# Layer 0's bias moved from the residual x to the half that the graph is applied to

## The chip, the cores and the metric

The kernel runs on one core of a Trainium2 chip. The metric is the device time of one execution in microseconds, lower is better. Five engines work side by side, each through its own queue in order: TensorE (PE: matmuls, and PEld: its weight loads), VectorE (DVE), ScalarE (ACT), GpSimd (POOL) and SyncE (SP), which starts the transfers. They wait for one another through semaphores.

## The reference

The input x has 64 batches of 256 nodes with 512 features; adj is a symmetric 256 x 256 graph of zeros and ones. Two residual layers with a layer norm follow each other. Layer 0 is a graph convolution, layer 1 masked attention with 8 heads of 64:

```python
Wi, Wj = (W[:, :Din], W[:, Din:])
mi = jnp.einsum('bkd,od->bko', x, Wi)
mj = jnp.einsum('bkd,od->bko', x, Wj)
a = adj.astype(x.dtype)
deg = a.sum(axis=1)
out = deg[None, :, None] * (mi + b) + jnp.einsum('ij,bjo->bio', a, mj)
...
x = _layernorm(x + _L0_gnn_ref(x, adj, L0_gnn_W, L0_gnn_b), axis=-1)
x = _layernorm(x + _L1_gnn_ref(x, adj, Wq, bq, Wk, bk, Wv, bv, Wo, bo), axis=-1)
```

The bias b of layer 0 comes in as deg times b. Since deg is the row sum of a, deg times b is also the graph applied to a matrix whose rows are all b: deg * (mi + b) + a @ mj equals deg * mi + a @ (mj + b).

## The kernel before

Everything is in float32, except the graph product. A tile has 128 partitions; one batch of x is `xh`, [128, 2, 512], two row tiles t. Batches go in pairs (NB = 2), 32 groups g. All large products are done in seven block products in place of eight, with sums of blocks made beforehand (`xS`, `hS`, `oS` hold S1 to S4) and factors of the weights made beforehand (`w0` for layer 0, streamed `factor` tiles for layer 1).

The main loop over g overlaps layer 1 of group g with layer 0 of group g+1. In a round, attention goes over eight pairs of heads, two at a time: `values` (pav) for the last two, `divide_two` (den on PE, the reciprocal L882 on DVE, the transfers to `spread`, later the aoT product on POOL, L844), `scores` (ps on PE; the mask add L805 on DVE, the exponential L809 on ACT, pk L812 on POOL). Between these stand the pieces of layer 0 of the next pair, from `l0_steps`; then come the output product, the finishing norms, and q, k, v of the next group. Matmuls and most calls marked `in_order` keep the order in which they are written; each engine runs its queue in order.

For one batch, `l0_steps` has seven products into four banks of PSUM, x, w, y and z, and then the graph:
- step 1 and 3 fill bank x (u1 is its copy on ACT, L530, and x's sum is added into xh, scaled by the degree, on DVE, L520); step 2 fills bank w, added into xh likewise.
- step 4 fills y; u2 = y + u1 on DVE (L542).
- step 5 fills z; the first half of the second row tile of mj is copied out of z by ACT (L547).
- step 6 adds to y; u3 = y + u1 on DVE (L551); mj's second row tile gets u3 added on POOL (L552); u3, scaled, is added into xh (L520).
- step 7 adds to z; the first row tile of mj is z + u2 on DVE (L561).
- after a row tile of mj, `split` makes hi (a rounded copy on ACT, L524) and lo (the rest, on POOL, L525).
- `neighbours` multiplies the graph with hi and lo (bank pa); `take` adds pa into xh (L575) and starts the norm.

Step 7 goes into the bank that step 5's copy reads, so it waits for that copy. `sum_x` makes xS of the second batch of a pair with four DVE operations (L477 to L480) just after step 7 of the first batch.

The bias comes into x: `degb` is deg times b, made once on DVE (L371); `add_bias` adds it to xh of each batch on POOL (L374), before layer 0 adds its products. b itself is a broadcast tile `b_bc` from a shared pool.

Of the kernel before, what the change touches and what calls it, by code (L numbers as in the profile page):

```python
# [8 lines left out]
F32 = mybir.dt.float32  # L9
# [3 lines left out]
ALU = mybir.AluOpType  # L13
# [3 lines left out]
P = 128  # L17
# [207 lines left out]
def unshifted_path(ctx, tc, flag, x, adj, wiT, wjT, b0, wqT, bq, wkT, bk, wvT, bv, woT, bo, out):  # L225
# [16 lines left out]
    nc = tc.nc  # L242
    B, N, D = x.shape
    NT = N // P
# [3 lines left out]
    NB = 2  # L248
    NG = B // NB
# [6 lines left out]
    const = ctx.enter_context(tc.tile_pool(name="const", bufs=1))  # L256
# [3 lines left out]
    p4 = ctx.enter_context(tc.tile_pool(name="p4", bufs=4))  # L260
# [8 lines left out]
    def bank(name):  # L269
        return ps_m.tile([P, 512], F32, tag="mm", name=name)  # L270

    def score_banks(name):
        return ps_s.tile([P, 2, 512], F32, tag="sc", name=name)
# [8 lines left out]
    def in_order(ins):  # L282

        tc.keep_in_program_order(ins)
# [4 lines left out]
    def matmul(*args, **kw):  # L289
        in_order(nc.tensor.matmul(*args, **kw))  # L290
# [5 lines left out]
    xh = {}  # L296
# [3 lines left out]
            xh[b] = p6.tile([P, NT, D], F32, tag="xh", name="xh")  # L300
            nc.sync.dma_start(out=xh[b], in_=x[b].rearrange("(t p) d -> p t d", p=P))

    b_bc = p4.tile([P, D], F32, tag="u", name="b_bc")
    xB, hB = {}, {}

    def load_xB(b):
# [31 lines left out]

    graph = const.tile([P, NT, N], F32R, name="graph")
    maskT = const.tile([P, NT, N], F32, name="maskT")  # L340
    degb = const.tile([P, NT, D], F32, name="degb")
    a = p2.tile([P, NT, N], F32, tag="pe", name="a")
    aT = p3.tile([P, NT, N], F32, tag="pk", name="aT")
    deg = small.tile([P, NT], F32, tag="deg", name="deg")
# [16 lines left out]
    def check_graph():  # L361
# [3 lines left out]
        in_order(nc.vector.tensor_tensor(exact, aT, graph.bitcast(F32), ALU.not_equal))  # L365
        in_order(nc.vector.tensor_reduce(inexact, exact.rearrange("p t n -> p (t n)"), AX.X, ALU.max))
        in_order(nc.vector.tensor_scalar(maskT, aT, 0.0, MASK, ALU.is_equal, ALU.mult))

    def degree_bias():
        for t in range(NT):  # L370
            in_order(nc.vector.tensor_scalar(degb[:, t, :], b_bc, deg[:, t:t + 1], None, ALU.mult))  # L371

    def add_bias(b):
        in_order(nc.gpsimd.tensor_tensor(xh[b], xh[b], degb, ALU.add))  # L374


    def load_bias(b, name):
# [86 lines left out]
    def norm_apply(t, below, rstd, order=anywhere):  # L464
        shift = small.tile([P, 1], F32, tag="shift", name="shift")
        order(nc.scalar.activation(shift, below, AF.Identity, scale=rstd))  # L466
        order(nc.scalar.activation(t, t, AF.Identity, bias=shift, scale=rstd))  # L467
# [34 lines left out]
    def l0_steps(b):  # L502
        banks, k = {}, {}

        def product(name, left, n, first):
            if first:
                banks[name] = bank("po")
            for c in range(2):
                matmul(banks[name], left[:, c, :], w0[:, n, c, :], start=(first and c == 0),
                                 stop=(c == 1), skip_group_check=True)  # L510

        def raw(t, h):
            return xT[b][:, 2 * h:2 * h + 2, t * P:(t + 1) * P]

        def keeper(name):
            k[name] = p3.tile([P, D], F32, tag="lu", name=name)
            return k[name]

        def add_scaled(t, src):
            nc.vector.scalar_tensor_tensor(xh[b][:, t, :], src, deg[:, t:t + 1], xh[b][:, t, :],  # L520
                                           ALU.mult, ALU.add)

        def split(t):
            nc.scalar.copy(k["hi"][:, t, :], k["mj"][:, t, :])  # L524
            nc.gpsimd.tensor_tensor(k["lo"][:, t, :], k["mj"][:, t, :], k["hi"][:, t, :].bitcast(F32),  # L525
                                    ALU.subtract)

        def step1():
            product("x", raw(0, 0), B11, True)
            nc.scalar.copy(keeper("u1"), banks["x"])  # L530

        def step2():
            product("w", raw(1, 1), T4, True)
            add_scaled(1, banks["w"])

        def step3():
            product("x", raw(0, 1), B21, False)
            add_scaled(0, banks["x"])

        def step4():  # L540
            product("y", xS[b]["S2"], T2, True)
            nc.vector.tensor_add(keeper("u2"), banks["y"], k["u1"])  # L542

        def step5():
            product("z", xS[b]["S1"], T1, True)
            k["mj"] = p1.tile([P, NT, D], F32, tag="mj", name="mj")
            nc.scalar.copy(k["mj"][:, 1, :], banks["z"])  # L547

        def step6():
            product("y", xS[b]["S3"], T3, False)  # L550
            nc.vector.tensor_add(keeper("u3"), banks["y"], k["u1"])  # L551
            nc.gpsimd.tensor_tensor(k["mj"][:, 1, :], k["mj"][:, 1, :], k["u3"], ALU.add)  # L552

            k["hi"] = p1.tile([P, NT, D], F32R, tag="hi", name="hi")
            k["lo"] = p1.tile([P, NT, D], F32R, tag="lo", name="lo")
            split(1)
            add_scaled(1, k["u3"])

        def step7():
            product("z", xS[b]["S4"], B22, False)  # L560
            nc.vector.tensor_add(k["mj"][:, 0, :], banks["z"], k["u2"])  # L561
            split(0)

        stats = {}

        def neighbours():
            k["pa"] = score_banks("pa")
            for i in (1, 0):
                for n, (j, part) in enumerate((j, part) for j in (1, 0) for part in ("hi", "lo")):
                    matmul(k["pa"][:, i, :], graph[:, j, i * P:(i + 1) * P], k[part][:, j, :],  # L570
                           start=(n == 0), stop=(n == 2 * NT - 1))

        def take(t):
            r = xh[b][:, t, :]
            in_order(nc.vector.tensor_add(r, k["pa"][:, t, :], r))  # L575
            stats[t] = norm_stats(r, in_order)

        def give(t):
            norm_apply(xh[b][:, t, :], *stats[t], in_order)


        return [step1, step2, step3, step4, step5, step6, step7, neighbours, lambda: take(1), lambda: take(0),
                lambda: give(1), lambda: send_h(b, 1), lambda: give(0), lambda: send_h(b, 0)]

# [310 lines left out]
    def layer0(g):  # L895

        b1, b2 = NB * g, NB * g + 1

        def item(f, *args):
            return lambda: f(*args)  # L900

        p, q = l0_steps(b1), l0_steps(b2)
        return [p[:3] + [item(turn_x, b2)] + p[3:4],
                p[4:7] + [item(sum_x, b2), item(add_bias, b2)] + q[:1],
                p[7:10], p[10:] + q[1:3],
                q[3:6] + [item(turn_h, b1)] + q[6:7],
                q[7:], [item(turn_h, b2)]]

    def run(steps):
        for s in steps:  # L910
            s()
# [4 lines left out]
    def order_of(name):  # L916
        return [(name, n) for n in RIGHT]

    for g in range(-1, NG - 1):
        o, q, k, v = (order_of(name) for name in ("wo", "wq", "wk", "wv"))  # L920
# [18 lines left out]
    p, q = l0_steps(0), l0_steps(1)  # L939
    run([p[0], p[2], p[4], p[3]])  # L940
    turn_x(1, "hB")
    degree_bias()
    add_bias(0)
    turn_graph()
    run([p[1], p[5], q[0], p[6], q[2]])
    add_bias(1)
    sum_x(1)
    run(q[1:2] + p[7:11] + q[3:5] + p[12:13])
    make_factors(wqT, "wq", raw_q)
# [9 lines left out]
    k = second_late(qk_steps(0, kT, "kT", bk_sb, bkd, True))  # L959
# [13 lines left out]
    run(v[2:3])  # L973
    turn_x(2)
    sum_x(2)
    add_bias(2)
    run(v[3:5])
    make_factors(woT, "wo", raw_o)
    load_x(3)
# [2 lines left out]
    for g in range(NG - 1):  # L982
        load_x(NB * (g + 2))
        load_x(NB * (g + 2) + 1)
        work = layer0(g + 1)
        run(work[0])
        for w in range(2, NB * NC, 2):
            values(g, w - 2)
            values(g, w - 1)
            multiply()  # L990
            divide_two(g, w - 1)
            scores(g, w)()
            if w == 4:
                run(work[2])
            later = scores(g, w + 1)
            later()
            run(work[w // 2 if w < 4 else w // 2 + 1])
        w = NB * NC - 2
        values(g, w)
        values(g, w + 1)  # L1000
        multiply()
        o = o_steps(g)
        q = second_late(qk_steps(g + 1, qT, "qT", bq_sb, bqd))
        k = second_late(qk_steps(g + 1, kT, "kT", bk_sb, bkd, True))
        v = second_late(v_steps(g + 1, True))
        neighbours, take1, take0, give1, send1, give0, send0 = work[SLOTS + 1]
        divide_two(g, w + 1)
        run([o[0], neighbours, take1, take0, q[0], give1, send1, o[1], give0, send0, multiply,
             *left_steps(oS[g], in_order), k[0], q[1], k[1]])
        run(o[2:6] + work[SLOTS + 2] + [v[0], o[6], v[1]])  # L1010
        end = finish_steps(g)
        k = with_output_bias(g + 1, k)[2:]
        run(q[2:5] + end[:1] + q[5:6] + end[1:2] + q[6:7] + end[2:3] + k[:1] + end[3:4] + k[1:] + end[4:] + v[2:3])
        turn_x(NB * (g + 2))
        sum_x(NB * (g + 2))
        if g + 2 < NG:
            add_bias(NB * (g + 2))
        run(v[3:5])
        run([scores(g + 1, 0), scores(g + 1, 1)])
        run(v[5:])  # L1020
# [3 lines left out]
    g = NG - 1  # L1024
# [89 lines left out]
```

## Time and profile before

The median of three runs is 3117.14 us (3116.6 to 3118.32); the profiled execution has a span of 3113.4 us.

| Engine | Busy us | Share of the span | Instructions |
|---|---|---|---|
| PE | 3071.3 | 99% | 14598 |
| PEld | 2117.8 | 68% | 14598 |
| DVE | 2148.5 | 69% | 3234 |
| ACT | 1007.8 | 32% | 1925 |
| POOL | 1520.8 | 49% | 1255 |

The rows of operations that the change touches, from the groups by line (busy us in total, mean ns of one):

| Line | Engine | What | Times | Busy us | Mean ns |
|---|---|---|---|---|---|
| L374 | POOL | xh + degb, 128x1024 | 64 | 157.7 | 2464 |
| L547 | ACT | mj from bank z, 128x512 | 64 | 36.8 | 575 |
| L561 | DVE | mj = z + u2, 128x512 | 64 | 43.9 | 686 |
| L552 | POOL | mj + u3, 128x512 | 64 | 111.6 | 1743 |
| L812 | POOL | pk, 128x512 | 256 | 322.3 | 1275 |
| L371 | DVE | degb, 128x512 | 2 | 1.9 | 966 |

A busy share is a mean over the whole span. An engine's idle time says something about the total only where another engine, in the end PE, waits for it. In the timeline every row has a start (us from the start of the span), a length, the engine, the line, the operation with its tiles, and in brackets how long the engine was idle before it and what ended that.

### The profile page before, as it was taken

The numbers are of one execution on the slowest core, as the hardware profiler recorded it, in microseconds if no ns is written. First come the engines' busy times: TensorE is split into PE (matmuls) and PEld (weight loads), VectorE is DVE, ScalarE is ACT, GpSimd is POOL, SyncE is SP. The second block draws the span as 40 slices with busy tenths as digits, with TensorE's granted clock in tenths as the row PEclk, the third lists the DMA queues.
The fourth block names the chain that finished last, engine by engine and source line by source line (L and its number), as shares of the span: only waits on it lengthen the run. The fifth ranks groups of instructions, "written<-read, shape, count | busy, mean of one in ns | idle before, by whom it ended". The sixth has DMA issues, their size and how long they took to land. (4 is left out here: it accounts for less than half of the span.)

```text
span 3113.4 us, 42777 instructions
## 1 busy us (share of the span) xinstructions
PE 3071.3 (99%) x14598; PEld 2117.8 (68%) x14598; DVE 2148.5 (69%) x3234; ACT 1007.8 (32%) x1925; POOL 1520.8 (49%) x1255
## 2 busy tenths in 40 slices
PE   7999999999999999999999999999999999999998
PEld 5667766677766677666776667766677766677665
DVE  6776676766777667676667676667766667767665
ACT  2333333323333333333233332333333333323332
POOL 2544445544545445454454554454544546445453
PEclk9999999999999999999999999999999999999999
DMA  7345544455444555445553445544455444555333
GB/s 256 121 143 156 166 124 134 128 157 165 141 124 123 157 166 152 117 131 149 157 166 118 131 134 157 165 139 123 127 155 169 146 118 127 154 162 160 116 111 98
DMA packets 410395, 447.28 MB, mean 144 GB/s; under 512 B 40896, under 2 KB 300224, under 8 KB 409792
## 3 DMA queue, kind: packets, MB, share of 16 engines
q1 hardware_dynamic: 410176, 444.50, 48.3%
q8 instruction: 120, 1.97, 0.3%
q14 instruction: 99, 0.81, 0.1%
HBM read 340.79 MB, written 70.25 MB: 132 GB/s over the span
## 5 line engine op out<-in xcount | busy, mean ns | idle before, releaser
L461 POOL TENSOR_TENSOR rstd<-ve,mhalf 128x1 f32<-128x1 f32 x256 | 140.6, 554 | 724.3 <-DVE below L459 724.3
L812 POOL TENSOR_TENSOR pk<-pe 128x512 f32<-128x512 f32 x256 | 322.3, 1275 | 341.0 <-ACT pe L809 341.0
L290 PE MATMUL po<-w,xS 128*128 128x512 f32 x1024 | 470.4, 602 | 6.1 <-ACT mj L547 5.6
L290 PE MATMUL st<-hS,factor 128*128 128x256 f32 x2048 | 452.7, 379 | 1.2 <-DVE u L685 1.2
L290 PEld LDWEIGHTS st<-hS,factor 128*128 128x128 f32 x2048 | 388.4, 190 | 55.1 <-DVE u L685 1.6
L809 ACT ACTIVATE pe<-pe 128x1024 f32<-128x1024 f32 x256 | 270.8, 1058 | 379.2 <-DVE pe L805 379.2
L290 PE MATMUL st<-hT,factor 128*128 128x256 f32 x1536 | 360.7, 381 | 9.0 <-ACT u L711 8.4
L290 PE MATMUL po<-w,xT 128*128 128x512 f32 x768 | 352.3, 601 | 13.8 <-DVE xT L485 11.3
L290 PEld LDWEIGHTS po<-w,xS 128*128 128x128 f32 x1024 | 186.8, 190 | 252.2 <-issue 191.5
L290 PEld LDWEIGHTS st<-hT,factor 128*128 128x128 f32 x1536 | 289.0, 190 | 61.5 <-ACT u L711 20.8
L805 DVE TENSOR_TENSOR pe<-ps,maskT 128x1024 f32<-128x1024 f32 x256 | 297.8, 1194 | 35.3 <-PE ps L290 35.3
L882 DVE RECIPROCAL rden<-den 128x256 f32<-128x256 f32 x127 | 222.8, 1754 | 73.7 <-PE den L290 68.2
L290 PEld LDWEIGHTS po<-w,xT 128*128 128x128 f32 x768 | 143.9, 191 | 181.4 <-issue 163.0
L290 PE MATMUL ps<-qT,kT 64*128 64x256 f32 x2048 | 264.9, 392 | 0.0
L883 POOL TENSOR_TENSOR rtot<-rtot,rden 128x256 f32<-128x256 f32 x127 | 92.8, 730 | 330.2 <-DVE rden L882 330.2
L290 PE MATMUL pav<-pe,v_sb 128*64 128x256 f32 x2048 | 250.1, 386 | 1.9 <-ACT pe L809 1.8
L740 DVE TENSOR_TENSOR xh<-st,xh 128x512 f32<-128x512 f32 x186 | 144.5, 777 | 149.7 <-PE st L290 149.7
L290 PEld LDWEIGHTS pav<-pe,v_sb 128*64 128x64 f32 x2048 | 135.2, 136 | 154.2 <-issue 72.0
L290 PEld LDWEIGHTS ps<-qT,kT 64*128 64x128 f32 x2048 | 184.3, 186 | 78.2 <-issue 51.3
L290 PE MATMUL st<-factor,hS 128*128 128x256 f32 x1024 | 234.8, 382 | 0.0
L290 PE MATMUL st<-factor,oS 128*128 128x256 f32 x992 | 224.2, 379 | 0.0
L290 PEld LDWEIGHTS st<-factor,hS 128*128 128x128 f32 x1024 | 191.9, 190 | 35.4 <-issue 10.6
(115 smaller groups left out, 4657.0 us busy)
## 6 DMA issues: line engine op xcount, KB each, us to landing
xB<-in_x_dram SPq DMA_DIRECT2D x256, 128.0 KB, 3.9
xh<-in_x_dram SPq DMA_DIRECT2D x64, 512.0 KB, 4.4
factor<-wq SPq DMA_DIRECT2D x128, 256.0 KB, 4.4
factor<-wk SPq DMA_DIRECT2D x128, 256.0 KB, 2.7
factor<-wv SPq DMA_DIRECT2D x128, 256.0 KB, 2.7
spread<-rden SPq DMA_DIRECT2D x1016, 32.0 KB, 1.9
factor<-wo SPq DMA_DIRECT2D x124, 256.0 KB, 3.3
h_cols<-xh SPq DMA_DIRECT2D x124, 256.0 KB, 2.5
```

The source lines that it names most:

```text
L290: in_order(nc.tensor.matmul(*args, **kw))
L461: nc.gpsimd.tensor_tensor(rstd, ve, mhalf, ALU.pow)
L740: nc.vector.tensor_add(dst, src, dst)
L805: nc.vector.tensor_add(pe.rearrange("p j t q -> p j (t q)"), ps.rearrange("p j t q -> p j (t q)"), maskT.rearrange("p t q -> p (t q)").uns ...
L809: in_order(nc.scalar.activation(flat, flat, AF.Exp, scale=QSCALE, accum_out=etot[:, NB * g + i, pr:pr + 1]))
L812: nc.gpsimd.tensor_tensor(pk, pe[:, :, 0, :], pe[:, :, 1, :], ALU.add)
L882: nc.vector.reciprocal(rden, den)
L883: nc.gpsimd.tensor_tensor(rtot, rtot, rden, ALU.add)
```

## The change

The bias is added to mj instead, before the graph is applied to it. For the second row tile of mj it comes with the emptying of bank z in step 5, which so becomes an addition on DVE in place of a copy on ACT. For the first row tile it is added to u2, on POOL, in step 4; step 7 then adds u2 as before. degb and add_bias go, and b_bc gets a buffer of its own, since it is now read to the end. The aim is to drop a large POOL addition of 1024 columns in each batch for a smaller one of 512 and no more work on the way out of PSUM.

```diff
-    b_bc = p4.tile([P, D], F32, tag="u", name="b_bc")
+    b_bc = const.tile([P, D], F32, name="b_bc")
...
-    degb = const.tile([P, NT, D], F32, name="degb")
...
-    def degree_bias():
-        for t in range(NT):
-            in_order(nc.vector.tensor_scalar(degb[:, t, :], b_bc, deg[:, t:t + 1], None, ALU.mult))
-
-    def add_bias(b):
-        in_order(nc.gpsimd.tensor_tensor(xh[b], xh[b], degb, ALU.add))
...
         def step4():
             product("y", xS[b]["S2"], T2, True)
             nc.vector.tensor_add(keeper("u2"), banks["y"], k["u1"])
+            nc.gpsimd.tensor_tensor(k["u2"], k["u2"], b_bc, ALU.add)
 
         def step5():
             product("z", xS[b]["S1"], T1, True)
             k["mj"] = p1.tile([P, NT, D], F32, tag="mj", name="mj")
-            nc.scalar.copy(k["mj"][:, 1, :], banks["z"])
+            nc.vector.tensor_add(k["mj"][:, 1, :], banks["z"], b_bc)
...
-                p[4:7] + [item(sum_x, b2), item(add_bias, b2)] + q[:1],
+                p[4:7] + [item(sum_x, b2)] + q[:1],
```

The five other calls of degree_bias and add_bias, at the start and at the end of a round, go too.

More of the change, by code (lines that the diff above doesn't have):

```diff
@@ L941, in unshifted_path @@
     turn_x(1, "hB")
-    degree_bias()
-    add_bias(0)
     turn_graph()
     run([p[1], p[5], q[0], p[6], q[2]])
-    add_bias(1)
     sum_x(1)
@@ L975, in unshifted_path @@
     sum_x(2)
-    add_bias(2)
     run(v[3:5])
@@ L1015, in unshifted_path @@
         sum_x(NB * (g + 2))
-        if g + 2 < NG:
-            add_bias(NB * (g + 2))
         run(v[3:5])
```

## The prediction

> **What bounds the kernel now.** I read the engine table first, then what TensorE waits for, then the timeline of one of the 31 equal rounds (the one from 1535.4 us).
>
> ```profile
> PE 3071.3 (99%) x14598; PEld 2117.8 (68%) x14598; DVE 2148.5 (69%) x3234; ACT 1007.8 (32%) x1925; POOL 1520.8 (49%) x1255
> ```
>
> The list of waits of PE (total us, times, longest):
>
> ```profile
> PE st L290 <- ACT u L711: 8.4, 31, 0.3
> PE po L290 <- ACT mj L547: 5.6, 31, 0.2
> ```
>
> TensorE (PE) is the bound; POOL, ACT and DVE have idle time, so their busy sums are worth nothing by themselves. Two waits of PE come once in each of the 31 rounds: one for ACT's u (L711), one for ACT's mj (L547), and the change moves L547. The starts of the first layer-0 matmul in round 0 (95.83 us) and round 30 (2975.39 us) give a round of 2879.56/30 = 95.985 us.
>
> ```profile
> 1546.87 2.29 DVE L805 TENSOR_TENSOR pe<-ps,maskT 128x1024 f32<-128x1024 f32 x2
> ...
> 1546.98 3.70 PE L290 MATMUL po<-w,xS 128*128 128x512 f32 x8
> ...
> 1549.19 1.06 ACT L809 ACTIVATE pe<-pe 128x1024 f32<-128x1024 f32 x1
> ...
> 1549.66 0.19 PEld L290 LDWEIGHTS po<-w,xS 128*128 128x128 f32 x1 [0.24 <-issue]
> ...
> 1550.25 0.57 ACT L547 COPY mj<-po 128x512 f32<-128x512 f32 x1
> 1550.72 0.69 DVE L551 TENSOR_TENSOR u<-po,u 128x512 f32<-128x512 f32 x1 [1.56 <-PE po L290]
> 1550.87 0.30 PEld L290 LDWEIGHTS po<-w,xS 128*128 128x128 f32 x2 [1.01 <-ACT mj L547]
> ...
> 1551.74 1.72 POOL L552 TENSOR_TENSOR mj<-mj,u 128x512 f32<-128x512 f32 x1
> ...
> 1552.26 0.19 PEld L290 LDWEIGHTS po<-w,xT 128*128 128x128 f32 x1 [0.24 <-issue]
> ...
> 1552.89 0.69 DVE L561 TENSOR_TENSOR mj<-po,u 128x512 f32<-128x512 f32 x1 [0.54 <-PE po L290]
> ...
> 1553.50 0.41 DVE L477 TENSOR_TENSOR xS<-xT 128x256 f32<-128x256 f32 x1
> ...
> 1554.19 2.72 POOL L525 TENSOR_TENSOR lo<-mj,hi 128x512 fp32r<-128x512 f32 x2 [0.73 <-ACT hi L524]
> 1554.29 1.50 DVE L479 TENSOR_TENSOR xS<-xT 128x256 f32<-128x256 f32 x1
> ...
> 1555.71 1.49 DVE L480 TENSOR_TENSOR xS<-xT,xS 128x256 f32<-128x256 f32 x1
> ...
> 1557.12 1.74 DVE L882 RECIPROCAL rden<-den 128x256 f32<-128x256 f32 x1
> ```
>
> Columns: start, length, engine, line, work. Of the eight matmuls from 1546.98 the first four are step 5, which fills bank z; step 7 adds to that bank and may start only when z has been copied out. The copy stands on ACT behind two exponentials and runs 1550.25 to 1550.82. Loads of weights otherwise stand 0.43 us apart. From the one at 1549.66 to the xT load are five steps: due at 1551.81, it comes at 1552.26. So the wait costs 0.45 us, and not the 0.18 us that the wait list gives it (5.6/31). Starts of matmuls say the same: step 7's first comes 345 ns late and its second another 105 ns. DVE meanwhile finishes its second L805 at 1549.16 and sits idle 1.56 us until step 6 is there.
>
> [...]L479, of 0.42 us by itself, takes 1.50 us beside L525 and ends 0.28 us after it, while L805 (PSUM and SBUF) runs beside POOL's L812 undisturbed.
>
> **The change part by part.**
> 1. The eviction in step 5: ACT copy (575 ns, 64 times) becomes a DVE add of the bank and b_bc. Nearest row: L561, same shape and same kinds of input, 686 ns[...]. The changed kernel's order on DVE is u2, reciprocal, the two L805, this add, u3. In the first batch of the pair it starts when the second L805 ends (1549.16; step 5 ended at about 1549.0) and ends at about 1549.85. Step 7 is due at 1550.52, its first load at 1550.09: in time by 0.2 us or more. Behind it on DVE stands only u3, which waits for step 6 until 1550.72 anyway. Saving: 0.45 us in 31 rounds = 13.9 us. In the second batch ACT takes z at 1572.87 without delay, and DVE is idle there from 1571.90 to 1574.59: 0.
> 2. add_bias goes: 64 POOL adds of 2464 ns (157.7 us). It is hidden: DVE waited for it once (1.8 us, in the start), and the aoT product behind it has 30 us until L477 of oS needs it. It counts only as room on POOL.
> 3. u2 += b_bc is new: 64 POOL adds. Same shape on POOL: 1275 ns (L812) if alone, 1743 ns (L552) when it must wait for DVE. In the first batch u2 is there at 1544.32 and POOL idle until 1547.03: hidden, since its reader L561 comes at 1552.4. In the second it follows the two L812, which end at 1573.94, and mj's add (L552) stands behind it:
>
> ```profile
> 1575.42 1.80 POOL L552 TENSOR_TENSOR mj<-mj,u 128x512 f32<-128x512 f32 x1 [1.48 <-DVE u L551]
> ```
>
> The idle time of 1.48 us holds 1.28 us. If it took 1.74 us, L552 would come 0.26 us late, but L552 is held up until about 1576.0 by DVE's L520 (two SBUF inputs) anyway. I take 0, at worst 0.3 us for hi and lo; the last lo ends at 1580.71 and PE needs it at 1581.18.
> 4. b_bc in a buffer of its own and degb gone: no wait in a round. At the start degb (1.85 us on DVE) goes; mj's add, the step-2 add and u3's scaled add move ahead of turning x of the second batch. That turning is what PE waits for at 25.35 us, and would come about 0.7 us later. Against it, L478 at 33.94, held 2.5 us by POOL's degb add and followed by a PE wait at 36.49, is freed. I take 0, between -1 and +1 us.
>
> Now whether the 0.45 us lasts. The first things after it are paced by PE and move with it, with one exception: DVE must end L480 before the reciprocal, and L805 after that frees the banks for the next scores at 1560.06. The reciprocal starts 0.446 us after the last den matmul where DVE is free, and 0.485 us after it here, so this chain is already level with PE to 0.04 us. L561 moves to 1552.44, L477 to 1553.05, where POOL's mj add holds the port until 1553.47 (its end, call it M, does not move: it follows pk and u3). A held DVE instruction ends 0.28 us after the POOL one: L477 at M+0.28, L478 from M+0.32, L479 from M+0.66. The first lo starts at M+0.73, after ACT's hi. So L479 is ahead by 70 ns; in the kernel before it is 92 ns behind and loses. Then L479 ends at M+1.08, lo at M+2.21 (1.13 us after the DVE instruction that held it, as three of them do now), L480 at M+2.49 = 1555.96, and the reciprocal is free at 1556.67, 0.45 us earlier. The second lo ends near 1557.1, needed at 1558.35. The gain stays.
>
> Sum: 3117.14 - 13.9 + 0 = 3103.2 us.
>
> **Rivals.**
> - The port goes to POOL's lo (the 70 ns are too few). Then L479, both lo and L480 end as before (L480 at 1557.15 or 1557.20), the reciprocal and L805 do not move, and PE waits at the scores for what it won at step 7, less 0.05 us: 3117.14 - 1.5 = 3115.6. For it: the level chain. Against: L479's earlier start.
> - POOL becomes the bound of the second batch: the new add and its port waits push mj, hi and lo. If all of 1.27 us showed, the last lo would end at 1581.98 against a need at 1581.18: PE loses 0.8 and wins 0.45, +0.35 in 31 rounds = 3128. Against: the 1.48 us hole.
> - The freed POOL also relieves the other wait of PE, for L711's u, which follows rstd on POOL. From the starts it costs 0.53 us a round; half of it would give 3095. Against: add_bias stood nowhere near it, and the POOL work in front of that rstd (aoT, rtot, L746, L747) is unchanged.
> - Half of the gain, with L479 ahead in some rounds only: 3110.
>
> **How the numbers follow.** Forecast 0.68; port lost 0.15; half 0.06; POOL bound 0.07; relief 0.04. A measurable gain (below 3110.9) is the forecast, the relief and most of the half: 0.77; same 0.15; slower 0.08. The range runs from 3100 (forecast with the start 1 us better and a little relief) to 3117 (port lost), so that the slower case and part of the relief, about 0.1, stay outside.
>
> **What would show it.** Right: the wait of PE for mj is gone from its list, the round is 95.54 us, L479's mean on xS falls from 940 ns to near 430 (half of its 64 runs are the held ones) while L480's 939 stays, and the first batch's reciprocal starts 0.45 us after den's last matmul. Wrong: the round stays at 95.98 and PE's scores wait for L805 (port), or neighbours' matmuls wait for POOL's lo (POOL bound), or step 7 waits for the new DVE add.

## The result and the profile after

The changed kernel takes 3137.82 us (median of 4 runs, 3136.68 to 3139.14) against 3117.0 us for the kernel before on the same chip: a ratio of 1.0066, 95% interval 1.0049 to 1.0084. It is slower by about 21 us, where 14 us less had been forecast.

Lines stand 7 or 8 earlier in the new kernel: the emptying (eviction) of bank z is L540 (was L547), the four xS additions are L469 to L472 (L477 to L480), the reciprocal is L875 (L882), ACT's u is L704 (L711), u3 is L544 (L551), mj's add on POOL is L545 (L552), the scaled add is L512 (L520), hT's turning is L477 (L485), z + u2 is L554 (L561), hi and lo are L516 and L517 (L524 and L525). The new u2 += b_bc is L535.

The engine table of the changed kernel:

```profile
PE 3071.3 (98%) x14598; PEld 2118.3 (68%) x14598; DVE 2189.4 (70%) x3296; ACT 967.7 (31%) x1861; POOL 1438.3 (46%) x1255
```

POOL has lost 82 us of work and ACT 40; DVE has gained 41: the emptying of z is 44, the scaled adds of u3 have grown by 35 (52.5 to 87.9) and L471 on xS has fallen by 33 (60.2 to 26.8). PE has the same instructions and the same busy time. So the 21 us are waits of PE, and the list of its waits (total us, times, longest) says which:

```profile
PE st L290 <- ACT u L704: 17.9, 31, 0.6
PE pa L290 <- POOL lo L517: 15.8, 31, 0.5
```

The wait for ACT's mj is gone, as it should be. A new wait has come in each of the 31 rounds, of the graph's matmuls (pa) for POOL's lo, and the wait for ACT's u has doubled. The rounds, between the first layer-0 matmuls of round 0 (96.85 us) and round 30 (2995.11 us), are now 2898.26/30 = 96.609 us, 0.624 more than before. Of the 21.3 us between the spans, 1.0 is a later start of round 0, 18.7 (30 times 0.624) are in the rounds up to the thirtieth, and 1.6 follow.

The starts of matmuls in one round (the sixteenth) split this up: 0.44 us won before the second batch's graph matmuls; 0.79 lost among these (one that reads lo starts 0.91 us after the one ahead of it instead of 0.23, the next 0.34 instead of 0.23); 0.30 lost at the wait for u (0.95 in place of 0.65). Together +0.65.

**First batch of the pair.** The timeline of the changed kernel there (start, length, engine, line, work; in brackets the idle time before and what ended it):

```profile
1559.44 0.68 DVE L540 TENSOR_TENSOR mj<-po,b_bc 128x512 f32<-128x512 f32 x1
...
1564.50 0.42 DVE L471 TENSOR_TENSOR xS<-xT 128x256 f32<-128x256 f32 x1
1564.57 2.90 POOL L517 TENSOR_TENSOR lo<-mj,hi 128x512 fp32r<-128x512 f32 x2 [0.73 <-ACT hi L516]
1564.84 1.50 DVE L472 TENSOR_TENSOR xS<-xT,xS 128x256 f32<-128x256 f32 x1
...
1567.00 1.76 DVE L875 RECIPROCAL rden<-den 128x256 f32<-128x256 f32 x1 [0.66 <-PE den L290]
```

L471 starts 70 ns ahead of lo and keeps its 0.42 us, and lo takes 1.49 us in place of 1.27; so in all 31 rounds, with leads of 67 to 72 ns. ("The port" in the prediction and the expectations is the author's name for what the trace shows in such a meeting of DVE and POOL: one of the two keeps its own length, the other ends only after it. That what they share is a port was not shown.) The reciprocal then waits for PE's den and for nothing else. The 0.45 us are there, and stay.

**Second batch.** First the kernel before, in its timeline (POOL's L552, at 1575.42 for 1.80 us, is the line shown in the prediction):

```profile
1574.59 0.69 DVE L551 TENSOR_TENSOR u<-po,u 128x512 f32<-128x512 f32 x1 [2.69 <-PE po L290]
...
1575.32 0.75 DVE L520 SCALAR_TENSOR_TENSOR xh<-u,deg,xh 128x512 f32<-128x512 f32 x1
...
1575.98 2.18 DVE L485 STREAM_TRANSPOSE hT<-hB 128x1024 f32<-128x1024 f32 x1
...
1578.01 0.70 DVE L561 TENSOR_TENSOR mj<-po,u 128x512 f32<-128x512 f32 x1
...
1579.44 1.27 POOL L525 TENSOR_TENSOR lo<-mj,hi 128x512 fp32r<-128x512 f32 x1 [0.21 <-ACT hi L524]
```

The same stretch of the changed kernel:

```profile
1583.84 1.27 POOL L535 TENSOR_TENSOR u<-u,b_bc 128x512 f32<-128x512 f32 x1
...
1584.52 0.69 DVE L544 TENSOR_TENSOR u<-po,u 128x512 f32<-128x512 f32 x1 [1.02 <-PE po L290]
...
1585.25 1.86 DVE L512 SCALAR_TENSOR_TENSOR xh<-u,deg,xh 128x512 f32<-128x512 f32 x1
1585.29 1.27 POOL L545 TENSOR_TENSOR mj<-mj,u 128x512 f32<-128x512 f32 x1 [0.19 <-DVE u L544]
...
1587.03 2.14 DVE L477 STREAM_TRANSPOSE hT<-hB 128x1024 f32<-128x1024 f32 x1
...
1589.07 0.66 DVE L554 TENSOR_TENSOR mj<-po,u 128x512 f32<-128x512 f32 x1
...
1590.45 1.28 POOL L517 TENSOR_TENSOR lo<-mj,hi 128x512 fp32r<-128x512 f32 x1 [1.87 <-ACT hi L516]
...
1591.78 0.50 PE L290 MATMUL pa<-lo,graph 128*128 128x512 f32 x1 [0.52 <-POOL lo L517]
```

Two instructions wait for u3: DVE's scaled add, with two inputs in SBUF, and POOL's add to mj. Before, the DVE one took 0.75 us and the POOL one was stretched to 1.80. Now POOL takes 1.27 and DVE is stretched to 1.86. That is the whole difference: 1.11 us on DVE. Behind the scaled add DVE has to turn hT and then to do z + u2, in order. From the start of u3 to the start of z + u2 it took 3.42 us before and takes 4.55 now; hi and lo follow. Since this batch begins 0.44 us earlier, lo ends 0.65 us later in the round than before (45.71 us after the round's start, before 45.06), and PE wants it 0.44 us sooner (at 45.53 before, so at 45.09 now). The 0.47 us to spare have become 0.62 us of delay. POOL itself goes on from there with aoT, rtot, two adds to xh and rstd, all 0.65 us later, and ACT's u hangs on that rstd. PE itself is only 0.34 us later there, so the second wait grows by the other 0.3.

Why did the order turn? The trace's list of mj's add on POOL in the kernel before, L552:

```profile
L552 POOLq EVENT_SEMAPHORE  x64: 17/17/43, 23.3 to 3015.1; - x64
L552 POOL TENSOR_TENSOR mj<-mj,u x64: 1281/1726/1800, 23.5 to 3015.2; 128x512 f32<-128x512 f32 x64
```

and in the changed kernel, L545 (columns: times; shortest, median and longest ns; first and last start):

```profile
L545 POOL TENSOR_TENSOR mj<-mj,u x64: 1262/1492/1766, 23.5 to 3034.4; 128x512 f32<-128x512 f32 x64
L545 POOLq EVENT_SEMAPHORE  x1: 17/17/17, 46.4 to 46.4; - x1
```

(EVENT_SEMAPHORE is the record of a separate wait, 17 ns at the median; POOLq is POOL's queue.) The add waited for two engines before, ACT (which had emptied z into mj) and DVE (u3), and all 64 adds have a separate wait in POOL's queue. With z emptied by DVE, the add waits for DVE alone, and the separate wait is gone from 63 of 64 adds. POOL's add then starts 79 ns after the end of u3 in place of 144, while DVE's starts 35 ns after it in both kernels. DVE's lead has shrunk from 109 ns to 44, and in all 32 meetings at 43 to 45 ns POOL goes first: its add takes 1.26 to 1.27 us, DVE's 1.85 to 1.86.

The changed kernel even holds its own exception, in the start, where the separate wait is left, at 46.4 us; the timeline there:

```profile
46.42 0.75 DVE L512 SCALAR_TENSOR_TENSOR xh<-u,deg,xh 128x512 f32<-128x512 f32 x1
46.53 1.77 POOL L545 TENSOR_TENSOR mj<-mj,u 128x512 f32<-128x512 f32 x1 [1.68 <-DVE u L544]
```

Here the lead is 110 ns, and DVE goes first (0.75 us, POOL's add 1.77). In the first batch of every round the add has lost its separate wait too, but it stands on POOL right behind pk and starts some 300 ns (297 to 313) after DVE's; there DVE goes first in all 31 rounds (0.89 to 0.90 us, POOL's add 1.72 to 1.73). So a missing wait alone doesn't turn the order: it did where it left the two starts some 44 ns apart.

### The profile page after: what moved, and what is told of

Its sections match the earlier page's. It is cut to its first block, busy times and chain, and to the rows that moved or that the text cites. A ratio compares the mean times of both kernels' runs of the same rounds, so it can differ in the third digit from the quotient of the medians.

```text
span 3134.7 us, 42751 instructions
## 1 busy us (share of the span) xinstructions
PE 3071.3 (98%) x14598; PEld 2118.3 (68%) x14598; DVE 2189.4 (70%) x3296; ACT 967.7 (31%) x1861; POOL 1438.3 (46%) x1255
## 5 line engine op out<-in xcount | busy, mean ns | idle before, releaser
L290 PE MATMUL po<-w,xS 128*128 128x512 f32 x1024 | 462.6, 599 | 0.0
L290 PE MATMUL st<-hT,factor 128*128 128x256 f32 x1536 | 360.8, 381 | 18.6 <-ACT u L704 17.9
L875 DVE RECIPROCAL rden<-den 128x256 f32<-128x256 f32 x127 | 223.0, 1756 | 92.1 <-PE den L290 88.9
L517 POOL TENSOR_TENSOR lo<-mj,hi 128x512 fp32r<-128x512 f32 x128 | 175.0, 1377 | 112.5 <-ACT hi L516 112.5
```

Of the source, the lines that this page charges most:

```text
L875: nc.vector.reciprocal(rden, den)
```

## The experiments

Theory (the lost wait): the emptying of z by DVE takes a wait from POOL's add, POOL goes first after u3, and DVE's 1.1 us do the rest. Rivals: POOL's new add to u2 is what delays lo; or DVE's extra 0.69 us is; or the bias's new place matters in some other way.

**e1: DVE empties z, the bias stays in x.** The kernel before, with one line changed:

```diff
-            nc.scalar.copy(k["mj"][:, 1, :], banks["z"])
+            nc.vector.tensor_copy(k["mj"][:, 1, :], banks["z"])
```

> The kernel before, with only the emptying of bank z moved from ACT to DVE (a plain copy); the bias stays in x. Lost-wait theory (mj's add on POOL now waits for one semaphore less, starts 65 ns sooner after u3[...]): the second batch of each pair loses as in the changed kernel, round about 96.6 us, time 3130 to 3137. POOL-load theory (the new u2 add on POOL does the harm): the first batch's 0.45 us is won and nothing is lost, round 95.54, time about 3103.

Measured: 3136.32 us (3135.88 to 3137.01), ratio 1.0061 (1.0045 to 1.0078), round 96.62 us. PE's waits:

```profile
PE st L290 <- ACT u L711: 18.0, 31, 0.6
PE pa L290 <- POOL lo L525: 16.1, 31, 0.5
```

and in the second batch's timeline:

```profile
1584.86 1.86 DVE L520 SCALAR_TENSOR_TENSOR xh<-u,deg,xh 128x512 f32<-128x512 f32 x1
1584.90 1.27 POOL L552 TENSOR_TENSOR mj<-mj,u 128x512 f32<-128x512 f32 x1 [1.41 <-DVE u L551]
```

The whole loss is here without the bias having moved at all: POOL has no add to u2, and sits idle 1.41 us ahead of L552. So neither that add nor the bias's place makes the loss.

**e2: the changed kernel, with ACT emptying z.**

```diff
-            nc.vector.tensor_add(k["mj"][:, 1, :], banks["z"], b_bc)
+            nc.scalar.copy(k["mj"][:, 1, :], banks["z"])
```

> The changed kernel with bank z again copied out by ACT; the bias is left out of the second row tile of mj, the u2 add on POOL stays and the degree-bias add stays away. Lost-wait theory: mj's add waits for two semaphores again, DVE keeps the port first, round 95.98 as before the change, time 3116 to 3119. POOL-load theory: the second batch loses about 1.07 us a round and the first wins nothing, round about 97.0, time about 3150.

Measured: 3118.47 us (3116.9 to 3121.64), ratio 1.0004 (0.9995 to 1.0013). Its wait list for mj and u is that of the kernel before again:

```profile
PE st L290 <- ACT u L704: 8.5, 31, 0.3
PE po L290 <- ACT mj L540: 5.6, 31, 0.2
```

and in the second batch the old order is back:

```profile
1575.65 0.75 DVE L512 SCALAR_TENSOR_TENSOR xh<-u,deg,xh 128x512 f32<-128x512 f32 x1
1575.76 1.79 POOL L545 TENSOR_TENSOR mj<-mj,u 128x512 f32<-128x512 f32 x1 [0.25 <-DVE u L544]
```

This kernel leaves the bias out of the second row tile of mj, so its output is not the reference's; it serves for the time alone. The round is 96.04 us, for 95.98 expected. POOL's add to u2 is in every batch and costs nothing that shows in the total. Together with e1: the change's effect, within about 2 us, lies in who empties z.

**e3: the changed kernel with the second wait put back.** ACT copies one column of mj onto itself after DVE's add, so that POOL's add has to wait for ACT as well as for DVE. DVE's work stays as in the changed kernel.

```diff
             nc.vector.tensor_add(k["mj"][:, 1, :], banks["z"], b_bc)
+            nc.scalar.copy(k["mj"][:, 1, 0:1], k["mj"][:, 1, 0:1])
```

> The changed kernel with one needless ACT copy of a single column of mj onto itself after the DVE add, so that mj's add on POOL again waits for two semaphores. Lost-wait theory: POOL starts some 144 ns after u3 instead of 79, DVE's scaled add gets the port, round about 95.54, time 3102 to 3106, faster than both kernels by adding work. POOL-load theory: no change from the changed kernel, round 96.6, time 3136 to 3140.

Measured: 3103.29 us (3102.5 to 3103.91), ratio 0.9955 (0.9939 to 0.9972), round 95.533 us. PE has no wait for lo any more, and the one for u is that of before, 8.3 us. The timeline:

```profile
1568.53 0.75 DVE L512 SCALAR_TENSOR_TENSOR xh<-u,deg,xh 128x512 f32<-128x512 f32 x1
1568.64 1.79 POOL L546 TENSOR_TENSOR mj<-mj,u 128x512 f32<-128x512 f32 x1 [0.25 <-DVE u L545]
```

One more instruction, which does nothing but add a wait, makes the changed kernel 34.5 us faster. The separate wait is back (64 times on L546), POOL starts 144 ns after u3, and DVE wins all 33 close meetings. That DVE has 0.69 us more to do is no matter: this kernel has it too.

**e4: the scaled add out of the way.** In the second batch, the changed kernel adds u3 to xh only after the graph's matmuls, so that no DVE instruction with two SBUF inputs meets POOL's add and nothing stands between u3 and hT's turning on DVE.

```diff
-            add_scaled(1, k["u3"])
+            if not late:
+                add_scaled(1, k["u3"])
...
+            if late:
+                add_scaled(1, k["u3"])
...
-        p, q = l0_steps(b1), l0_steps(b2)
+        p, q = l0_steps(b1), l0_steps(b2, True)
```

> The changed kernel with the scaled add of u3 into xh (DVE) of the second batch moved behind the z + u2 add of step 7, so that no DVE instruction with two SBUF inputs stands beside mj's add on POOL. Lost-wait theory: turning h and z + u2 are no longer held up, the last lo is in time, round 95.54 or a little less, time 3095 to 3105. POOL-load theory: lo stays late since POOL has too much before it, time over 3125.

Measured: 3092.99 us (3091.88 to 3094.49), ratio 0.9921 (0.9905 to 0.9938), round 95.170 us. That is below the range expected: the loss is gone as foretold, but a second gain, in the wait for u, had not been counted. The second batch's timeline:

```profile
1565.94 2.13 DVE L477 STREAM_TRANSPOSE hT<-hB 128x1024 f32<-128x1024 f32 x1
1566.11 1.29 POOL L545 TENSOR_TENSOR mj<-mj,u 128x512 f32<-128x512 f32 x1 [0.19 <-DVE u L544]
...
1567.96 0.66 DVE L555 TENSOR_TENSOR mj<-po,u 128x512 f32<-128x512 f32 x1
1568.12 2.95 POOL L517 TENSOR_TENSOR lo<-mj,hi 128x512 fp32r<-128x512 f32 x2 [0.73 <-ACT hi L516]
1568.54 1.41 DVE L512 SCALAR_TENSOR_TENSOR xh<-u,deg,xh 128x512 f32<-128x512 f32 x1
```

hT's turning has one SBUF input and runs beside POOL's add, at 2.13 us (in the changed kernel 2.05 to 2.11 with nothing on POOL beside it) and 1.29 us (1.26 to 1.27 where the add went first there); the scaled add now waits for lo, where nobody waits for it. The two los end early enough for POOL to bring rstd forward, and PE's wait for u, present in both kernels, nearly goes: the matmul behind it starts 0.06 us late, where it was 0.43 in the kernel before. Round 0 begins at 99.23 us here, 2.4 later than in the changed kernel, though the edit leaves the start as it was. By 17.5 us e4 is already 1.9 us behind: four matmuls in a row start 0.85 us after the one ahead of them, where in the changed kernel it is 0.43. Why was not found. The starts of single profiled executions thus differ by more than the 1.0 us between the two kernels.

**e5: the late scaled add in the kernel before,** ACT still emptying z. The edit is that of e4.

> The kernel before, with the second batch's scaled add of u3 put behind its neighbours' matmuls and nothing else changed. Lost-wait theory, by which the two SBUF readers that meet after u3 set the second batch's time whichever of them wins: the copy of z on ScalarE still costs the first batch its 0.45 us a round, and the second batch's wait of TensorE for ScalarE's u (0.27 us of idle time a round, 8.4 us in all) goes, with the late add at about 1.4 us behind z plus u2. Round 95.17 + 0.45 = 95.62 us in place of 95.985, so 3117 - 0.365 x 31 = about 3106 us (3103 to 3110). Rival, that the late add paid in the changed kernel only because DVE had taken over the emptying of z: no gain here, 3115 to 3119 us.

Measured: 3107.5 us (3106.23 to 3108.89), ratio 0.9968 (0.9957 to 0.998), round 95.69 us (95.62 expected). So the late add pays with ACT emptying z as well, and the rival fell. The wait for u leaves PE's list and that for mj stays:

```profile
PE po L290 <- ACT mj L547: 5.7, 31, 0.2
```

**e6: e1 and e5 together,** the bias in x.

> The kernel before, with DVE's plain copy of z in place of ScalarE's and the late scaled add in the second batch; the bias stays in x by GpSimd. Lost-wait theory: the gains add up and the form of the bias is of no account in the rounds: round 95.17 us as in e4_late_add, no wait of TensorE for ScalarE's mj, for GpSimd's lo or for ScalarE's u above 0.1 us a round; with the start of the kernel before (first layer-0 matmul of the first round at about 96 us in place of e4's 99.2) about 3090 us (3087 to 3094). Rival, that moving the bias into layer 0 carries part of e4's gain (GpSimd freed of add_bias at another place of the round): round above 95.4 us and more than 3097 us.

Measured: 3090.51 us (3089.24 to 3092.67), ratio 0.9913 (0.99 to 0.9927), round 95.160 us against e4's 95.170. The 2.5 us between it and e4 are not explained by the rounds; the start of round 0 is 1.4 us earlier (97.84 us, not the 96 expected), which is no more than starts differ anyway. The gains add up: 0.45 us a round from the eviction (e3) and 0.29 from the late add (e5) against 0.83 here; of the 0.08 over, most is the wait for u, whose matmul is 0.12 us late in e5 and 0.06 in e6. With the late add the rounds are the same wherever the bias is added. e6 is faster than the kernel before and the changed one, and needs no new buffer for b_bc.

## Why the prediction was wrong

- *What bounds the kernel, and step 1's 0.45 us:* right. The wait for mj left PE's list, and e3, the changed kernel with one wait more, takes 3103.29 us, the forecast's 3103.2, with a round of 95.533 for the 95.54 foretold.
- *Step 1's addition, nearest row 686 ns:* right, L540 takes 686 ns, from 1559.44 on without a gap behind the second mask add.
- *Whether the 0.45 us lasts in the first batch, with L471 ahead of lo by 70 ns:* right, to the nanoseconds of the start. L471's mean on xS fell from 940 (as L479) to 418 ns and L472's stayed at 942 (939 as L480). The rival of the lost port fell. But what it took for granted, that the one with the earlier start in the trace goes first, fails at 44 ns in the same kernel; that it held at 70 ns was luck as much as working.
- *Steps 2 and 3, no cost for add_bias and u2 += b_bc:* right for the instructions themselves (e2 has neither add_bias nor degb, has the new add, and is the same as before; L535 takes 1275 ns).
- *Step 4, the start between -1 and +1:* round 0 begins 1.02 us later, just outside, but e4, with the same code up to there, begins it another 2.4 later; single executions don't settle this step.
- *The step that failed* is in the second batch, twice over. Step 1 set the change of the eviction at 0 there, because ACT took z without delay: it asked who waits for the eviction's end, and not which waits the eviction gives to its readers. And step 3 took for granted that "L552 is held up until about 1576.0 by DVE's L520 (two SBUF inputs) anyway". In the changed kernel L545 is held up by nothing, and L512 is held up by it, 1.86 us in place of 0.75. PE pays for it with 0.79 us at lo and 0.30 more at u in each round, where the sum had 0. The first batch's meeting was worked out to 70 ns, the second's was copied over.
- *The rival "POOL becomes the bound of the second batch"* gave 3128 us and named the right symptom, PE waiting for lo, with a wrong cause: it put it down to the added POOL instruction, which e1 does without at the same loss. That its 0.8 us of delay comes near the measured 0.79 is luck. The rival of relief, that a freer POOL shortens the wait for u, fell: that wait doubled, from 8.4 to 17.9 us.

What the traces show is that the one that goes second ends well after the other: DVE's scaled add 0.55 us after POOL's add (1.86 us long in place of 0.75), POOL's add 1.16 us after DVE's (1.80 us in place of 1.27). Which goes first can't be read off the starts in a trace: DVE's start is 43 to 45 ns the earlier in each of the 32 meetings that it lost in the changed kernel. No run here shows what decides it.

## What to carry to other kernels

When an instruction moves to another engine, write down for each of its readers which engines that reader waited for before and waits for after: a reader that loses its second engine can lose a separate wait and start earlier (65 ns on POOL here), and this was enough to turn the order of two instructions of which one holds up the other (1.11 us on DVE here). Where two such instructions follow the same event, compare their leads with ones that the trace has shown to win, and count both outcomes, with what is queued behind the loser; here the changed kernel's work takes 3103 us in one order (e3) and 3138 in the other. Better than to tune the order is to move the one that nobody needs yet out of the meeting, as e4 and e6 do.

## What the runs showed of the hardware

- The separate wait on POOL delays its instruction by 65 ns (144 ns after DVE's end in place of 79), though the record of it is 17 ns long.
- After the end of a common DVE instruction, DVE's two-input instruction went first with starts 106 ns or more ahead of POOL's (33 of 33 in e2 and in e3, 31 of 31 in the kernel before) and second with 43 to 45 ns (32 of 32 in the changed kernel, 31 of 31 in e1). In the first batch L471, itself behind another DVE instruction, went first with 67 to 72 ns against lo (31 of 31 in the changed kernel). So these runs give no threshold that holds for any two instructions; leads between 45 and 106 ns after u3 were not tried, and what decides the order is not shown.
- A wait of PE cost more than its idle time shows: 0.52 us shown at lo, 0.79 by the starts of matmuls, of which 0.11 at the matmul after the late one (sixteenth round of the changed kernel).
